# A four-layer graph network on one core: three of four transposes moved from TensorE to VectorE and DRAM, two sums begun on GpSimd, weights loaded by the plan

## The chip, the cores and the metric

The kernel runs on one core of one Trainium2 chip. The metric is the time of one execution in microseconds of device time, the median of several runs. Engines are named as in the profile: PE (TensorE matmuls), PEld (its weight loads), DVE (VectorE), ACT (ScalarE), POOL (GpSimd), SP (SyncE, which here only issues DMAs).

## The reference, cut to what matters

There are 64 independent graphs of 256 nodes with 256 features, and four layers in a row, each of the form `x = layernorm(x + gnn(x, adj))`. All is float32.

```python
# layer 0, 4 heads of 64
att = sigmoid(einsum('bhxd,bhyd->bhxy', q, k) * scale)      # q, k, X: leaky_relu(x @ W)
adj_h = adj[:, None] * att;  deg = sum(adj_h, -1);  dis = where(deg > 0, deg ** -0.5, 0)
Y = einsum('bhxy,bhyd->bhxd', dis[..., :, None] * adj_h * dis[..., None, :], X)    # then layernorm
# layer 1, 8 heads of 32: masked softmax attention, then @ Wo
# layer 2: agg = eps * x + adj @ x;  h = silu(rmsnorm(agg @ W1 + b1));  out = h @ W2 + b2   (1024 hidden)
# layer 3: Wh = x @ W; e = leaky_relu(s1 + s2); out = gelu(layernorm(masked softmax(e) @ Wh))
```

## The kernel before, in words

**Tiles.** One graph's x is a tile of 128 partitions by 512 numbers (two blocks of 128 nodes, side by side). A matmul contracts over partitions, so layers 0, 1 and 3 need x with features on partitions, `xT`. Layer 0 gets it from the input, which is also given transposed. Four times per graph the kernel transposes on PE: `transpose` (L184) issues four 128x128 matmuls against an identity (L189) into PSUM. They are the heads' output of layer 0 (`yT`, L361), x ahead of layer 1 (`xT`, L371), x ahead of layer 3 (`xT3`, L511) and the attention weights of layer 3 (`eT`, L538). `copy` (ACT, L199) fetches a PSUM tile to SBUF. The heads' attention weights of layer 1 go another way already: DVE transposes blocks of 32x32 (L400), SP writes the result to a scratch buffer in DRAM (L402, `far<-eb`) and reads it back in another order with four DMAs (L404, `eT<-far`), in runs of 1 KB.

**Two sums on PE.** Layer 0's degree is a product with a column of ones (L333), over both blocks of nodes of four heads: eight matmuls, packed four side by side in PE's columns. Layer 2's sum of squares is the same (L470), in two runs of four matmuls on the four `sq` tiles that ACT squares (L464).

**A planner.** `graph` records the operations of one graph with an engine, a cost in ns and the tiles they write and read. `Plan.order` sorts the operations of all 64 graphs by list scheduling: the operation that can start first goes next, ties go to the earlier due time. It holds the numbers of buffers per kind (`SLOTS`: 42 of kind `s`, 8 PSUM banks, 8 DRAM buffers), and ACT's functions in turns so that a function table is loaded once per layer and round. `ROUND = 0, 2, 4, 5` says how many rounds behind layer 0 each layer of the same graph runs; about six graphs are under way at any time. The order that results is fixed in the program: each engine, and SP's queue too, runs its instructions in that order and waits on semaphores. A DMA counts 420 ns of SP and lands 4500 ns later in the plan's books.

**Weights** are fetched ahead of the plan by 23 DMAs that ACT issues (`weight`, `row`, `column`, L584 to L621). `c1`, `w3` and `eps_id` are computed from them, `c1` with the program's first matmul (L631).

Of the kernel before, what the change touches and what calls it, by code (L numbers as in the profile page):

```python
# [28 lines left out]
ROUND = 0, 2, 4, 5  # L29
# [3 lines left out]
class Value:  # L33
# [3 lines left out]
    def __init__(self, kind, name, parts=1):  # L37
        self.kind, self.name = kind, name
        self.writer, self.readers = [None] * parts, [[] for _ in range(parts)]
        self.uses, self.slot, self.end, self.t = 0, None, 0.0, None  # L40

# [121 lines left out]

def graph(plan, nc, c, t, out, b):
# [31 lines left out]

    def copy(ps, name):
        dst = Value("s", name, 2)
        op("ACT", 466, lambda: act.copy(dst.t, ps.t), [dst], [ps])  # L199
        return dst  # L200

    def feature_major(w, xT):

        ps = Value("p", "ps", 2)
        for o in range(2):
            def fn(o=o):
                for k in range(DB):
                    pe.matmul(two(ps)[:, o, :], w()[:, k, o * P:(o + 1) * P], two(xT)[:, k, :],  # L208
                              start=(k == 0), stop=(k == DB - 1))
            op("PE", 2 * PE_MM, fn, [(ps, o)], [xT])  # L210
        return ps
# [49 lines left out]
    def plus_row(x, r):  # L261
        xb = Value("s", "xb", 2)
        op("POOL", 1220, lambda: pool.tensor_tensor(two(xb), two(x), row_b(r()), OP.add), [xb], [x])  # L263
        return xb
# [6 lines left out]
    def affine(y, mv, m, g, add, r=(), src=None):  # L271

        src = src or y
        for n in range(NB):
            op("DVE", 395, lambda n=n: dve.scalar_tensor_tensor(
                two(y)[:, n, :], two(src)[:, n, :], m()[:, n, 0:1], g(), op0=OP.subtract, op1=OP.mult),
                [(y, n)], [(src, n), mv])
# [21 lines left out]
    for w, name in ((lambda: c.w0_q, "qT0"), (lambda: c.w0_k, "kT0")):  # L299
# [5 lines left out]
    ps = token_major(xT, lambda: c.w0_l)  # L305
    v = Value("s", "v0")
    op("DVE", 608, lambda ps=ps: dve.tensor_tensor(two(v), two(ps), row_b(c.b0_l), OP.add), [v], [ps])
    op("ACT", 478, lambda: act.activation(v.t, v.t, AF.Prelu, alpha=0.01), [v], [v])
    xb = plus_row(x, lambda: c.b0)
# [18 lines left out]
    ps = Value("p", "ps")  # L328

    def fn(ps=ps):  # L330
        for m in range(NB):
            for h in range(H0):
                pe.matmul(ps.t[h * 32:(h + 1) * 32, :N], c.ones, A(h)[:, m, :], start=(m == 0), stop=(m == NB - 1))  # L333
    op("PE", 2 * PE_MM, fn, [ps], [att], mode="columns")
# [18 lines left out]
    for hp in range(H0 // 2):  # L353
# [7 lines left out]
    ps = transposed(copy(ps, "yT"))  # L361
    y = Value("s", "y", 2)
    op("DVE", 608, lambda ps=ps, y=y: dve.tensor_tensor(by_head(y.t), by_head(ps.t), dis_b(), OP.mult), [y], [ps, dis])
    mv, m = stats(y)
    affine(y, mv, m, lambda: c.g0, lambda n, xb=xb: two(xb)[:, n, :], [xb])
# [5 lines left out]
    xT = copy(transposed(x), "xT")  # L371
    xb = plus_row(x, lambda: c.c1)
    ps = feature_major(lambda: c.w1_q, xT)
    qT1 = Value("s", "qT1")
    op("DVE", 608, lambda ps=ps: dve.tensor_tensor(two(qT1), two(ps), c.b1_q[:, :, None].to_broadcast([P, 2, N]), OP.add),
       [qT1], [ps])

    kT1 = copy(feature_major(lambda: c.w1_k, xT), "kT1")
    v1 = copy(token_major(xT, lambda: c.w1_v), "v1")
# [51 lines left out]
    x = normed(plus(token_major(yT, lambda: c.w1_o), xb), "x2")  # L431

    for n in range(NB):
        d = lambda n=n: two(adjT)[:, n, n * P:(n + 1) * P]
        op("POOL", 418, lambda d=d: pool.tensor_tensor(d(), d(), c.eps_id, OP.add), [(adjT, n)], [(adjT, n)])


    xb = plus_row(x, lambda: c.b2_2)
# [12 lines left out]
    for j in range(0, HB, 2):  # L451
        ps = Value("p", "ps", 2)
        for i in range(2):
            def fn(ps=ps, j=j, i=i):
                for k in range(DB):
                    pe.matmul(two(ps)[:, i, :], c.w2_1[:, k, (j + i) * P:(j + i + 1) * P], two(aggT)[:, k, :],  # L456
                              start=(k == 0), stop=(k == DB - 1))
            op("PE", 2 * PE_MM, fn, [(ps, i)], [aggT])
        both = [(hT, j), (hT, j + 1)]
        for i in range(2):  # L460
            op("ACT", 357, lambda ps=ps, i=i, j=j: act.activation(  # L461
                Hb(j + i)[:, 0], two(ps)[:, i, :], AF.Identity, bias=c.b2_1[:, j + i:j + i + 1]), [(hT, j + i)], [(ps, i)])
# [4 lines left out]
        if len(sqs) == 2:  # L467
            def fn(sqs=sqs, j=j):
                for i in range(4):
                    pe.matmul(sums.t[i * 32:(i + 1) * 32, :N], c.ones, two(sqs[i // 2])[:, i % 2, :],  # L470
                              start=(j == 2), stop=(j == HB - 2))
            op("PE", PE_MM, fn, [sums], [sums, *sqs] if j > 2 else sqs, mode="columns")
            sqs = []
# [17 lines left out]
    for j in range(HB):  # L491
        op("DVE", 391, lambda j=j: dve.scalar_tensor_tensor(  # L492
            Hb(j)[:, 0], Hb(j)[:, 0], c.r2[:, j:j + 1], pr.t[:, :N], op0=OP.mult, op1=OP.mult), [(hT, j)], [(hT, j), pr])
# [5 lines left out]
    for n in range(NB):  # L499
        for half in range(2):  # L500
            js = range(4 * half, 4 * half + 4)

            def fn(ps=ps, n=n, js=js):
                for j in js:
                    pe.matmul(two(ps)[:, n, :], Hb(j)[:, 0, n * P:(n + 1) * P], c.w2_2[:, j, :],  # L505
                              start=(j == 0), stop=(j == HB - 1))
            op("PE", 4 * PE_MM, fn, [(ps, n)], [(hT, j) for j in js] + [(ps, n)] * half)
# [3 lines left out]
    xT3 = copy(transposed(x), "xT3")  # L511
# [3 lines left out]
    for n in range(NB):  # L515
        ps = Value("p", "ps")

        def fn(ps=ps, n=n):
            for k in range(DB):
                pe.matmul(ps.t[:, :D + 2], two(xT3)[:, k, n * P:(n + 1) * P], c.w3[:, k, :],  # L520
                          start=(k == 0), stop=(k == DB - 1))
        op("PE", 2 * PE_MM + 4, fn, [ps], [xT3])
# [19 lines left out]
    affine(y3, mv, m, lambda: c.g3, lambda n: c.b3, src=ps)  # L542
# [7 lines left out]
def gnn_stack_kernel(ctx: ExitStack, tc: tile.TileContext, t: dict, out: bass.AP):  # L550
# [32 lines left out]

    def weight(name):  # L584
        rows, cols = t[name].shape
        w = const.tile([P, rows // P, cols], F32, name=name)
        nc.scalar.dma_start(w, t[name].rearrange("(k p) f -> p k f", p=P))
        return w

    def row(ap, name):  # L590

        r = const.tile([P, ap.shape[0]], F32, name=name)
        nc.scalar.dma_start(r, bass.AP(tensor=ap.tensor, offset=ap.offset, ap=[[0, P], [1, ap.shape[0]]]))
        return r

    def column(ap, name):

        c = const.tile([P, ap.shape[0] // P], F32, name=name)
        nc.scalar.dma_start(c, ap.rearrange("(k p) -> p k", p=P))
        return c  # L600

    w0_q, w0_k, w0_l = weight("L0_gnn_W_q"), weight("L0_gnn_W_k"), weight("L0_gnn_W_lin")
    b0_l = row(t["L0_gnn_b_lin"], "b0_l")
    g0, b0 = row(t["L0_gnn_ln_g"], "g0"), row(t["L0_gnn_ln_b"], "b0")
    w1_q, w1_k, w1_v, w1_o = (weight(f"L1_gnn_W{c}") for c in "qkvo")
    b1_q, b1_v = column(t["L1_gnn_bq"], "b1_q"), column(t["L1_gnn_bv"], "b1_v")
    b1_o = row(t["L1_gnn_bo"], "b1_o")
    w2_1, w2_2 = weight("L2_gnn_W1"), weight("L2_gnn_W2")
    b2_1, r2 = column(t["L2_gnn_b1"], "b2_1"), column(t["L2_gnn_rms_weight"], "r2")
    b2_2 = row(t["L2_gnn_b2"], "b2_2")  # L610
    eps2 = row(t["L2_gnn_epsilon"], "eps2")
    g3, b3 = row(t["L3_gnn_gamma"], "g3"), row(t["L3_gnn_beta"], "b3")
    a3 = row(t["L3_gnn_a"].rearrange("a one -> (a one)"), "a3")


    eps_id = const.tile([P, P], F32, name="eps_id")
    nc.vector.tensor_scalar(eps_id, ident, eps2[:, 0:1], None, op0=OP.mult)


    w3 = const.tile([P, DB, D + 2], F32, name="w3")  # L620
    nc.scalar.dma_start(w3[:, :, :D], t["L3_gnn_W"].rearrange("(k p) f -> p k f", p=P))  # L621
    scratch = const.tile([P, D], F32, name="scratch")
    for k in range(DB):
        for i in range(2):
            nc.vector.scalar_tensor_tensor(scratch, w3[:, k, :D], 1.0, a3[:, i * D:(i + 1) * D], op0=OP.mult,
                                           op1=OP.mult, accum_out=w3[:, k, D + i:D + i + 1])


    ps = pools["p"].tile([P, 512], F32, tag="p", name="ps")[:, :D]
    for k in range(DB):  # L630
        nc.tensor.matmul(ps, b1_v[:, k:k + 1].to_broadcast([P, P]), w1_o[:, k, :], start=(k == 0), stop=(k == DB - 1))  # L631
    c1 = const.tile([P, D], F32, name="c1")
    nc.vector.tensor_tensor(c1, ps, b1_o, OP.add)
    c = SimpleNamespace(**locals())

    plan = Plan()
    for b in range(B):
# [45 lines left out]
```

## Time and profile before

| | |
|---|---|
| median of three runs | 3023.94 us (3023.19 to 3023.97) |
| the profiled execution | 3018.84 us, of which the instructions span 3017.0 us |
| PE / DVE / ACT / POOL busy | 97% / 74% / 67% / 33% of the span |
| DMA packets, mean rate | 305684, 126 GB/s |
| granted PE clock, mean | 0.993 |

The page gives busy shares per engine, then groups of instructions by source line. In a group, "busy" counts the time in which at least one instruction of it runs; "mean" is one instruction's own length. PE's matmuls overlap, so what one costs is read from the start of it to the start of the next. An fp32 matmul is two records in the trace, a transpose is one. "Idle before, releaser" is how long the engine stood still ahead of the group, and who ended it.

### The profile page before, as it was taken

How to read it: one execution, taken by the hardware profiler on the slowest of the kernel's cores; microseconds unless marked ns; L12 is line 12 of the kernel's file. 1: busy time of each engine (PE TensorE's matmuls, PEld its weight loads, DVE VectorE, ACT ScalarE, POOL GpSimd, SP SyncE). 2: the span in 40 equal slices, each digit the busy share in tenths (PEclk: the TensorE clock that was granted, in tenths of full speed). 3: DMA queues.
4: the chain of work that ended last, by engine and by line, in shares of the span. 5: the costliest groups of instructions: out<-in, count | busy, mean ns of one | idle time of the engine just before them, and what ended most of it. 6: DMA issues, size and time to landing. Idle time of an engine off the chain costs nothing.

```text
span 3017.0 us, 57099 instructions
## 1 busy us (share of the span) xinstructions
PE 2925.9 (97%) x19140; PEld 2281.5 (76%) x19140; DVE 2236.8 (74%) x6925; ACT 2019.2 (67%) x4866; POOL 1002.0 (33%) x1286
## 2 busy tenths in 40 slices
PE   6999999999999999999999999999999999999996
PEld 4777777777777777777777777777777877777774
DVE  3778877768777777787687777777777777777864
ACT  2777766776776667676767667667666766677664
POOL 4224333324323333333233323332332333323311
PEclk9999999999999999999999999999999999999998
DMA  5634543534543435434435344344344443553340
GB/s 162 175 102 141 151 123 113 144 105 130 155 131 101 130 109 144 139 118 140 130 95 146 107 134 148 109 137 143 97 133 137 124 126 106 141 141 112 106 126 11
DMA packets 305684, 378.79 MB, mean 126 GB/s; under 512 B 37872, under 2 KB 272240, under 8 KB 305392
## 3 DMA queue, kind: packets, MB, share of 16 engines
q1 hardware_dynamic: 297984, 369.76, 41.9%
q10 hardware_dynamic: 7408, 5.39, 0.6%
q8 instruction: 153, 2.51, 0.4%
q14 instruction: 139, 1.14, 0.1%
HBM read 223.49 MB, written 151.52 MB: 124 GB/s over the span
## 4 chain that ended last, share of the span: by engine, by line
PE 79%; DVE 10%; ACT 6%; DMA 3%; issue 1%; POOL 1%; SPq 0%; ACTq 0%; DVEq 0%; POOLq 0%
PE ps L208 14%; PE ps L219 13%; PE ps L456 12%; PE ps L505 12%; PE ps L388 4%; PE ps L189 3%; PE ps L443 3%; PE ps L358 3%; PE ps L319 3%; PE av L413 3%; PE ps L520 3%; ACT e L292 3%; PE sums L470 2%; DVE st L233 2%; PE ps L333 2%
## 5 line engine op out<-in xcount | busy, mean ns | idle before, releaser
L292 ACT ACTIVATE e<-e,low 128x256 f32<-128x256 f32 x1152 | 583.0, 510 | 67.5 <-DVE low L287 66.9
L456 PE MATMUL ps<-aggT,L_gnn_W 128*128 128x256 f32 x2048 | 487.6, 385 | 1.6 <-ACT aggT L199 1.3
L505 PE MATMUL ps<-L_gnn_W,hT 128*128 128x256 f32 x2048 | 469.0, 383 | 0.3 <-ACT hT L496 0.3
L400 DVE STREAM_TRANSPOSE eb<-e 128x1024 f32<-128x1024 f32 x256 | 316.2, 1237 | 170.5 <-ACT e L292 169.9
L456 PEld LDWEIGHTS ps<-aggT,L_gnn_W 128*128 128x128 f32 x2048 | 377.9, 191 | 81.1 <-issue 24.5
L505 PEld LDWEIGHTS ps<-L_gnn_W,hT 128*128 128x128 f32 x2048 | 385.0, 190 | 70.1 <-issue 19.3
L245 POOL TENSOR_SCALAR mv<-mv 128x2 f32<-128x2 f32 x384 | 125.0, 326 | 905.1 <-DVE mv L235 753.4
L287 DVE CUSTOM_DVE_ANT_0 e<-ps,adj 128x256 f32<-128x256 f32 x1024 | 363.3, 418 | 25.4 <-PE ps L388 25.0
L461 ACT ACTIVATE hT<-ps,b 128x256 f32<-128x256 f32 x512 | 234.2, 471 | 157.9 <-PE ps L456 157.9
L246 POOL TENSOR_TENSOR mv<-mv,mhalf 128x2 f32<-128x2 f32 x384 | 287.6, 749 | 32.0
L263 POOL TENSOR_TENSOR xb<-x,b 128x512 f32<-128x512 f32 x128 | 166.5, 1301 | 281.5 <-DMA x<-in_x 184.8
L233 DVE BATCH_NORM_STATS2 st<-y 128x6 f32<-128x256 f32 x640 | 242.8, 415 | 4.3
L292 ACT ACTIVATION_READ_ACCUMULATOR e<-e,low 128x1 f32 x1152 | 229.8, 199 | 0.0
L492 DVE SCALAR_TENSOR_TENSOR hT<-hT,r,pr 128x256 f32<-128x256 f32 x512 | 205.4, 473 | 20.8 <-PE pr L489 20.5
L326 DVE TENSOR_TENSOR att<-att,adjT 128x512 f32<-128x512 f32 x256 | 170.5, 697 | 21.3 <-ACT att L324 21.3
L256 DVE TENSOR_SCALAR x<-y,mv 128x256 f32<-128x256 f32 x384 | 163.2, 457 | 24.4 <-POOL mv L246 24.0
L484 POOL TENSOR_TENSOR rs<-rs,mhalf 128x2 f32<-128x2 f32 x64 | 46.1, 720 | 377.4 <-DVE rs L483 358.7
L464 ACT ACTIVATE sq<-hT 128x512 f32<-128x512 f32 x256 | 161.9, 633 | 0.3
L496 ACT ACTIVATE hT<-hT 128x1024 f32<-128x1024 f32 x128 | 131.6, 1053 | 40.4 <-DVE hT L492 31.8
L324 ACT ACTIVATE att<-ps 128x512 f32<-128x512 f32 x256 | 132.4, 603 | 27.2 <-PE ps L505 22.4
L346 POOL TENSOR_TENSOR dp<-dp,mhalf 128x8 f32<-128x8 f32 x64 | 107.6, 1682 | 126.1 <-DVE dp L345 119.8
L219 PE MATMUL ps<-v,eT 128*128 128x256 f32 x512 | 141.4, 408 | 8.3 <-ACT eT L199 3.7
(108 smaller groups left out, 5901.1 us busy)
## 6 DMA issues: line engine op xcount, KB each, us to landing
far<-eb SPq DMA_DIRECT2D x256, 512.0 KB, 3.2
eT<-far SPq DMA_DIRECT2D x1024, 128.0 KB, 3.8
x0T<-in_xT SPq DMA_DIRECT2D x64, 256.0 KB, 3.5
adjT<-in_adjT SPq DMA_DIRECT2D x64, 256.0 KB, 3.8
x<-in_x SPq DMA_DIRECT2D x64, 256.0 KB, 3.9
adj<-in_adj SPq DMA_DIRECT2D x64, 256.0 KB, 3.9
rb<-far SPq DMA_DIRECT2D x512, 32.0 KB, 1.9
out<-o SPq DMA_DIRECT2D x64, 256.0 KB, 2.2
```

The lines of the kernel that those rows point to most:

```text
L208: pe.matmul(two(ps)[:, o, :], w()[:, k, o * P:(o + 1) * P], two(xT)[:, k, :], start=(k == 0), stop=(k == DB - 1))
L219: pe.matmul(two(ps)[:, n, :], two(xT)[:, k, n * P:(n + 1) * P], w()[:, k, :], start=(k == 0), stop=(k == DB - 1))
L233: op("DVE", 311, lambda n=n: dve.bn_stats(st.t[:, 6 * n:6 * n + 6], two(src)[:, n, :]), [(st, n)], [(src, n)])
L246: pool.tensor_tensor(m()[:, :, 2], m()[:, :, 2], c.mhalf[:, :NB], OP.pow)
L287: op("DVE", 345, lambda n=n: dve.tensor_tensor_reduce(out=E(n), in0=two(logits)[:, n, :], in1=two(negmask)[:, n, :], scale=-scale, scalar= ...
L292: op("ACT", 491, lambda n=n: act.activation(E(n), E(n), AF.Exp, bias=low.t[:, n:n + 1], scale=-1.0, accum_out=r.t[:, col(n):col(n) + 1]), ...
L326: op("DVE", 608, lambda h=h: dve.tensor_tensor(A(h), A(h), two(adjT), OP.mult), [(att, h)], [(att, h), adjT])
L400: op("DVE", 1130, lambda e=e, eb=eb: dve.transpose(eb.t.rearrange("p (b g i) -> p g b i", b=4, i=32), e.t.rearrange("p (g b i) -> p g b i" ...
L456: pe.matmul(two(ps)[:, i, :], c.w2_1[:, k, (j + i) * P:(j + i + 1) * P], two(aggT)[:, k, :], start=(k == 0), stop=(k == DB - 1))
L461: op("ACT", 357, lambda ps=ps, i=i, j=j: act.activation(Hb(j + i)[:, 0], two(ps)[:, i, :], AF.Identity, bias=c.b2_1[:, j + i:j + i + 1]), ...
L492: op("DVE", 391, lambda j=j: dve.scalar_tensor_tensor(Hb(j)[:, 0], Hb(j)[:, 0], c.r2[:, j:j + 1], pr.t[:, :N], op0=OP.mult, op1=OP.mult), ...
L505: pe.matmul(two(ps)[:, n, :], Hb(j)[:, 0, n * P:(n + 1) * P], c.w2_2[:, j, :], start=(j == 0), stop=(j == HB - 1))
```

## The change

1. `yT`, `xT` and `xT3` no longer go through PE and ACT's `copy`, but through `far_transposed`: one DVE transpose of 32x32 blocks (of `yT` straight from PSUM), a write to DRAM, four DMAs back. For `yT` it is one write of 2 KB rows and four reads in runs of 512 B, and the rows' order within the tile is left permuted: the multiplication by `dis` that follows (two instructions of 256 numbers now, one of 512 before) puts it right. For `xT` and `xT3` it is four writes in runs of 512 B and four reads in runs of 128 B. `eT` of layer 3 stays on PE.
2. POOL adds pairs of tiles ahead of the two sums: two additions per graph for the degree, two for the sum of squares. PE then does four matmuls in place of eight for each.
3. The weights are operations of the plan and are issued by SP between the inputs' loads, by due time; no DMA is left on ACT.
4. `ROUND` is 0, 2, 5, 7.

```diff
-ROUND = 0, 2, 4, 5
+ROUND = 0, 2, 5, 7
...
+def weights(plan, nc, c, t):
...
+    def weight(name, key, rows=D, cols=D):
+        v = const(name, [P, rows // P, cols])
+        op("SP", rows * cols // 200 + 420, lambda: nc.sync.dma_start(
+            v.t, t[key].rearrange("(k p) f -> p k f", p=P)), [v], after=3500)
...
+    def far_transposed(src, name, in_order=True):
+
+
+        eb, far, dst = Value("s", "eb"), Value("h", "far", 4), Value("s", name, 4)
+        op("DVE", 600, lambda: dve.transpose(
+            eb.t.rearrange("p (b g i) -> p g b i", b=4, i=32),
+            src.t.rearrange("p (n k w) -> p k n w", n=2, k=2)), [eb], [src])
+        if in_order:
+            F = lambda a: far.t[:64].rearrange("(a z) (y w) -> a (z y) w", a=4, w=P)[a]
+            for a in range(4):
+                op("SP", 420, lambda a=a: nc.sync.dma_start(
+                    F(a).rearrange("(b j) w -> j b w", b=4),
+                    eb.t[32 * a:32 * a + 32].rearrange("j (b w) -> j b w", b=4)), [(far, a)], [eb], after=3000)
+            for a in range(4):
+                op("SP", 420, lambda a=a: nc.sync.dma_start(
+                    dst.t.rearrange("q (g a i) -> a q g i", g=4, a=4)[a],
+                    F(a).rearrange("q (g i) -> q g i", g=4)), [(dst, a)], [(far, a)], after=4500)
+            return dst
+        op("SP", 420, lambda: nc.sync.dma_start(far.t[:, :512], eb.t), [(far, i) for i in range(4)], [eb], after=3000)
+        for q in range(4):
+            op("SP", 420, lambda q=q: nc.sync.dma_start(
+                dst.t[32 * q:32 * q + 32].rearrange("j (a g) -> j a g", a=4),
+                far.t[:, :512].rearrange("(a j) (b g) -> b j a g", a=4, b=4)[q]), [(dst, q)],
+                [(far, i) for i in range(4)], after=4200)
+        return dst
...
+    added = [Value("s", "added") for _ in range(H0 // 2)]
+    for i in range(2):
+        A2 = lambda n, i=i: att.t.rearrange("p (h n c) -> p h n c", h=H0, n=NB)[:, 2 * i:2 * i + 2, n]
+        op("POOL", 1220, lambda i=i, A2=A2: pool.tensor_tensor(two(added[i]), A2(0), A2(1), OP.add),
+           [added[i]], [(att, 2 * i), (att, 2 * i + 1)])
...
-        for m in range(NB):
-            for h in range(H0):
-                pe.matmul(ps.t[h * 32:(h + 1) * 32, :N], c.ones, A(h)[:, m, :], start=(m == 0), stop=(m == NB - 1))
-    op("PE", 2 * PE_MM, fn, [ps], [att], mode="columns")
+        for h in range(H0):
+            pe.matmul(ps.t[h * 32:(h + 1) * 32, :N], c.ones, two(added[h // 2])[:, h % 2], start=True, stop=True)
+    op("PE", PE_MM, fn, [ps], added, mode="columns")
...
-    ps = transposed(copy(ps, "yT"))
+    yb = far_transposed(ps, "yT", in_order=False)
...
-    xT = copy(transposed(x), "xT")
+    xT = far_transposed(x, "xT")
...
+        if len(sqs) % 2 == 0:
+            op("POOL", 1220, lambda a=sqs[-2], sq=sq: pool.tensor_tensor(sq.t, sq.t, a.t, OP.add), [sq], [sq, sqs[-2]])
...
-    xT3 = copy(transposed(x), "xT3")
+    xT3 = far_transposed(x, "xT3")
```

More of the change, by code (lines that the diff above doesn't have):

```diff
@@ L262, in plus_row @@
         xb = Value("s", "xb", 2)
-        op("POOL", 1220, lambda: pool.tensor_tensor(two(xb), two(x), row_b(r()), OP.add), [xb], [x])
+        op("POOL", 1220, lambda: pool.tensor_tensor(two(xb), two(x), row_b(r.t), OP.add), [xb], [x, r])
         return xb
@@ L370, in graph @@
     negmask = adj
[L371 to L373 removed]
+    xT = far_transposed(x, "xT")
+    xb = plus_row(x, c.c1)
+    ps = feature_major(c.w1_q, xT)
     qT1 = Value("s", "qT1")
[L375 to L379, printed above, removed]
+    op("DVE", 608, lambda ps=ps: dve.tensor_tensor(two(qT1), two(ps), c.b1_q.t[:, :, None].to_broadcast([P, 2, N]), OP.add),
+       [qT1], [ps, c.b1_q])
+    kT1 = copy(feature_major(c.w1_k, xT), "kT1")
+    v1 = copy(token_major(xT, lambda: c.w1_v.t, [c.w1_v]), "v1")
     av, r = Value("p", "av", 2), Value("c", "r")
@@ L465, in graph, with fn @@
         sqs.append(sq)
[L467 to L473, printed above, removed]
+        if len(sqs) % 2 == 0:
+            op("POOL", 1220, lambda a=sqs[-2], sq=sq: pool.tensor_tensor(sq.t, sq.t, a.t, OP.add), [sq], [sq, sqs[-2]])
+    def fn(sqs=sqs):
+        for i in range(4):
+            pe.matmul(sums.t[i * 32:(i + 1) * 32, :N], c.ones, two(sqs[i // 2 * 2 + 1])[:, i % 2, :],
+                      start=True, stop=True)
+    op("PE", PE_MM, fn, [sums], [sqs[1], sqs[3]], mode="columns")
     part = Value("s", "part")
@@ L602, in gnn_stack_kernel @@
[L602 to L632, printed above, removed]
@@ L633, in gnn_stack_kernel @@
-    nc.vector.tensor_tensor(c1, ps, b1_o, OP.add)
-    c = SimpleNamespace(**locals())
+    c = SimpleNamespace(const=const, ident=ident, ones=ones, mean_of=mean_of, mhalf=mhalf)
     plan = Plan()
+    weights(plan, nc, c, t)
     for b in range(B):
```

108 lines of the change are left out of this document (73 added, 35 removed).

## The prediction

> **What bounds the kernel now.** I read the page first: busy shares, then the chain of work that ended last.
>
> ```profile
> PE 2925.9 (97%) x19140; PEld 2281.5 (76%) x19140; DVE 2236.8 (74%) x6925; ACT 2019.2 (67%) x4866; POOL 1002.0 (33%) x1286
> ...
> PE 79%; DVE 10%; ACT 6%; DMA 3%; issue 1%; POOL 1%; SPq 0%; ACTq 0%; DVEq 0%; POOLq 0%
> ```
>
> PE is busy almost throughout and the chain runs over it, so what is taken off PE should come off the time, as far as no other queue takes its place. Next, busy time by stretches (columns: us, then PE, PEld, DVE, ACT, POOL busy with instruction counts, granted clock, DMA share, GB/s):
>
> ```profile
> 0.00:40.00 40.00, 11.45 (x42) 9.20 (x44) 0.83 (x5) 4.81 (x7) 16.60 (x16) 0.88 0.94 289
> 40.00:60.00 20.00, 20.00 (x136) 15.34 (x134) 13.48 (x27) 9.70 (x19) 11.48 (x10) 0.99 0.10 34
> 60.00:2900.00 2840.00, 2806.32 (x18521) 2190.32 (x18518) 2164.60 (x6708) 1941.55 (x4707) 956.49 (x1229) 1.00 0.44 127
> 2900.00:3005.00 105.00, 87.99 (x450) 66.60 (x449) 52.32 (x169) 62.49 (x134) 15.54 (x27) 0.91 0.17 51
> 3005.00:3017.00 12.00, 0.14 (x1) 0.00 (x0) 5.57 (x18) 0.63 (x1) 1.86 (x4) 0.50 0.06 23
> ```
>
> PE stands still 28.6 us of the first 40, 33.7 of the 2840 between, and 28.9 of the last 117. DMA has room in the middle, none at the start. Then PE's timeline, where a line's cost is the distance to the next line's start:
>
> ```profile
> 1616.10 0.30 PE L189 MATMUL ps<-ident,x 128*128 128x128 f32 x1 [0.80 <-DVE x L256]
> 1616.93 0.55 PE L189 MATMUL ps<-ident,x 128*128 128x128 f32 x3 [0.53 <-DVE x L256]
> ...
> 1621.03 1.05 PE L333 MATMUL ps<-att,ones 128*32 128x256 f32 x16
> 1622.01 0.66 PE L189 MATMUL ps<-ident,x 128*128 128x128 f32 x4
> 1622.50 0.60 PE L189 MATMUL ps<-ident,yT 128*128 128x128 f32 x4
> 1622.94 0.38 PE L341 MATMUL ps<-ident,deg 128*128 128x128 f32 x2
> ```
>
> Four transposes of x cost 0.49 us here (mean of all 128 runs 0.52, waits apart), four of yT 0.44, the degree's sum 0.98. From the groups and the DMA view:
>
> ```profile
> L189 PE MATMUL ps<-ident,x 128*128 128x128 f32 x512 | 84.1, 282 | 23.4 <-DVE x L256 23.2
> L400 DVE STREAM_TRANSPOSE eb<-e 128x1024 f32<-128x1024 f32 x256 | 316.2, 1237 | 170.5 <-ACT e L292 169.9 <-DMA rb<-far 0.2
> L256 DVE TENSOR_SCALAR o<-y,mv 128x256 f32<-128x256 f32 x128 | 63.9, 541 | 17.8 <-POOL mv L246 17.8
> L413 PE MATMUL av<-eT,v 128*32 128x256 f32 x2048 | 125.5, 382 | 0.0
> far<-eb SPq DMA_DIRECT2D x256, 512.0 KB, 3.2
> eT<-far SPq DMA_DIRECT2D x1024, 128.0 KB, 3.8
> ```
>
> The first row's 23.2 us are PE waiting for DVE ahead of x's transposes. L413, which reads tiles that went through DRAM, never waited: the plan's 4500 ns cover the 3.8 us measured.
>
> **PE, work removed.** Transposes of x: 128 x 0.52 = 66 us. Of yT: 64 x 0.44 = 28. Degree: half of eight matmuls is two of four packed passes of 216 ns (the start-to-start median of a 256-column record), 64 x 0.43 = 28. Sum of squares: one of two runs goes. A run of eight records takes 0.58, and the matmul ahead of it takes 309 ns in place of 216, so 64 x 0.67 = 43. Sum **165 us**, all on the path. The 23 us of waiting at L189 go too; their successor is below.
>
> **Start, moved.** Before, PE's first matmul waits 18.4 us for `b_v`, and ACT issues weights until 34.8, so its first activation comes then. After, SP issues `W_q`, `W_k` and three x0T first; `W_q` landed 3.8 us after issue before, so PE starts near 5. Against that, all 23 weight loads now stand in SP's queue: the first `yT` write is 47th in its order, and 11.6 MB at the 289 GB/s above take 40 us. Until layer 1's first matmul, the order holds 56 us of layer 0 on PE, and that matmul can hardly come before 70. I take 18 us idle for 28.6, a gain of **10**, with ends 25 and -10.
>
> **End.** The last graph's x now takes the way through DRAM ahead of layer 3 with nothing beside it: DVE 0.6, last write issued 1.4 later (three issues of 0.48, start to start), landing 3.2, last read 3.8, together 9.1, for 2 us of transposes and copy; one POOL addition (1.3) ahead of the sum of squares; and two more rounds between layer 0 and layer 3 leave PE less to do beside the last chains. A chain some 8 longer plus about 11 us of cover lost: **19 us**, ends 5 and 45.
>
> **DVE.** Added: 192 transposes of half of L400's 1.24, 119 us (yT's reads PSUM, which no transpose here does yet; L363 reads as much from there in 0.68, so at most 4 more), and 10 to 18 for the split multiplication. POOL gets 256 additions of 1.30 (row of L263), 333 us, to 1335, under half the span. They hurt DVE: L256 has a median of 407 ns but a mean of 541 and a longest of 1395, and the long ones lie beside POOL's 1.3 us operations. Such excess sums to some 51 us now over 383 us of POOL's long operations; 333 more bring 44. DVE comes to 2410 of 2860 us, 84%: not the bound. The Trainium skill (SBUF — State Buffer, SBUF: two separate sides) says that GpSimd and a two-port DVE operation exclude each other for a whole instruction, which is what L256 shows; by that rule, if each new addition held DVE for half its length, an estimate of 166 us in place of 44, DVE would stand at 89%. ACT loses 192 copies of 0.58, 112 us.
>
> **DMA and SP.** Per graph there are 21 DMAs more: 5760 data packets, 4096 of them of 128 B, 1536 of 512 B, 128 of 2 KB. The packet records of before have 9.4 ns for loads of 4 B, 32.9 for 512 B, 60.6 for 1 KB and 180 for 4 KB (means). A 128 B packet lies between 9.4 and, far off, 60.6; I take 18, nearer the first two. Then the 128 B runs add 295 us per engine (154 to 993), the rest 260; with today's 1297 the DMA share is 65% (60 to 89%). Here the Trainium skill speaks against the change (DMA: Bandwidth & Descriptors, Specifications): under 512 B the engine does a read-modify-write. The 4 B loads at 9.4 ns do not show that; if such a packet cost twice the 512 B one, an estimate of 66 ns, the share would be about 92%. SP issues 55 DMAs per graph for 34, 25 us at today's 0.39 to 0.48; with waits for landings, some 4.7 pairs of write and read per graph with little between, 32 of 44.6 us. Nothing is gained by issue time; it must stay hidden.
>
> **New waits.** What counts is PE work standing, in the new order, between a chain's matmul and the matmul that reads its result (counted at 216 ns per record). From layer 0's attention product over yT, two normalizations and xT to layer 1's first product: 34 to 35 us. By rows the chain is 9.1 (DRAM) + 8.1 (16 DVE and 4 POOL steps) + 9.1 (DRAM) = 26.3; the middle part is the multiplication 0.9, statistics 2 x 1.2, POOL 2 x 1.1, scale and add 1.9, scaling 0.8. For x3: 18 to 21 us against 3.8 + 9.1 = 12.9. Before, x3's chain of 3.8 had 5.3 to 6.1 and still caused most of the 23 us, so queueing on DVE eats about 2 us per such chain, and about 5 of x1's. That leaves x1's 3.3 us and x3's 3 to 6. Only tails should stall: I take twice today's 23, **46**, ends 0 and 170 (below).
>
> **Sum.** 3018.8 (profiled run) - 165 - 23 - 10 + 19 + 46 = 2886; the median of the runs lies 5 above the profiled one: **2890 us**.
>
> **Rivals.**
> *A, forecast*, PE stays the bound: 2850 to 2925. Chance 0.58.
> *B, landings lengthen a little.* x1's chain passes four landings. If each takes between 0.85 and 1.5 us more than 3.2 and 3.8, the 3.3 us are used up and each graph stalls for up to 4 x 1.5 - 3.3 = 2.7 us, 173 us in all: 2925 to 3017, middle 2970. For: SP's queue is in order, and a write waiting for DVE holds all reads behind it. Against: the new DMAs are light (0.3 to 0.7 us of the engines each, for 1.44 of an `eb` write). Chance 0.17.
> *C, slower.* The same chain becomes the bound: from about 1.5 us more per landing (5.3 where eT's median is 3.8 and its longest 6.9) the stalls exceed all that PE saved. At 2 us more, 64 x (4 x 2 - 3.3) = 301 us on top of the 2845 without waits: 3146. For: in the first 40 us, at a DMA share of 0.94, x0T landed up to 8.7 after issue. Against: it needs 128 B packets near 60 ns, which would bring the share to 89%. Chance 0.15.
> *D, the waits vanish and the start gains 25*: 2830 to 2850. Chance 0.07.
> *E, the change does not do what it says.* In the new order the records of L189 on x and yT are gone and the sums are halved, so it can only be that waits eat just that much: 3018 to 3030, chance 0.03.
>
> The range takes A, B and half of D: **2840 to 3015**. Faster by over 0.2% (about what a measurement of this kernel can tell from no change) 0.82, within it 0.03, slower 0.15.
>
> **What would show it.** PE busy near 2750 us; no L189 on x and yT; the two sums at half their records; PE's first matmul near 5 us; DVE's share near 84%; DMA near 65%, 128 B packets near 18 ns. Wrong would be: reads of 128 B landing over 5 us, PE waiting for DMA xT for more than 100 us in sum, or idle PE beyond 60 us at the end.

## The result, and the profile after

The change takes **3184.07 us** (median of four runs, 3177.18 to 3188.14) where the kernel before, on the same chip, takes 3023.95: ratio 1.0527 [1.0508, 1.0545]. It was forecast at 2890 and is slower by 5%. (One kernel further below, `weights`, ran slow while it was profiled, 3381.7 us at a granted clock of 0.845 where its nine other runs take about 3028, so its trace is not read.) The page of the changed kernel, busy times and the chain that ended last:

```profile
span 3182.6 us, 56140 instructions
...
PE 2898.6 (91%) x17348; PEld 2218.9 (70%) x17348; DVE 2467.2 (78%) x7181; ACT 1937.4 (61%) x4676; POOL 1326.8 (42%) x1542
...
PE 48%; DMA 16%; DVE 13%; ACT 9%; SPq 6%; POOL 4%; issue 2%; DVEq 0%; POOLq 0%; ACTq 0%
```

PE has 1792 records fewer, as planned, but only 27 us less busy time, and stands idle 284.0 us (span less busy) where it stood 91.1. DMA now carries 16% of the chain. Which wait it is, the list of PE's waits says (waiting line and tile, releaser: us in total, times, longest):

```profile
PE ps L303 <- DMA x0T<-in_xT: 127.6, 27, 6.0
PE sums L576 <- POOL sq L572: 33.0, 27, 1.7
PE ps L625 <- DMA xT<-far: 13.5, 4, 9.4
PE ps L432 <- POOL added L427: 13.0, 5, 6.1
```

The largest is not a transposed tile. It is `x0T`, layer 0's input, which is loaded as before: a load that the change does not touch. The same matmuls as groups of lines, in the kernel before, after, and (ahead of its turn) in the best mended version, `books_l12`:

```profile
L208 PE MATMUL ps<-x0T,L_gnn_W_q 128*128 128x256 f32 x512 | 126.5, 386 | 0.2 <-DMA x0T<-in_xT 0.2
```

```profile
L303 PE MATMUL ps<-x0T,w_q 128*128 128x256 f32 x512 | 173.2, 485 | 127.6 <-DMA x0T<-in_xT 127.6
```

```profile
L303 PE MATMUL ps<-x0T,w_q 128*128 128x256 f32 x512 | 129.8, 391 | 8.0 <-DMA x0T<-in_xT 8.0
```

Two things changed in the middle row: the idle time ahead, and the busy time itself (173.2 for 126.5) for the same 512 records. One of the 27 stalls shows both. SP's queue and PE, from the timeline of the changed kernel:

```profile
2056.12 6.75 SPq L508 DMA_DIRECT2D eT<-far  x10
2062.98 0.40 SPq L651 DMA_DIRECT2D out<-o  x1
2063.42 2.89 SPq L508 DMA_DIRECT2D eT<-far  x6
2066.41 0.40 SPq L250 DMA_DIRECT2D adj<-in_adj  x1
2066.85 0.47 SPq L250 DMA_DIRECT2D x0T<-in_xT  x1
```

```profile
2066.13 0.27 PE L524 MATMUL ps<-ident,r 128*16 128x128 f32 x1
2071.67 2.04 PE L303 MATMUL ps<-x0T,w_q 128*128 128x256 f32 x4 [5.26 <-DMA x0T<-in_xT]
```

The load is issued at 2066.85, when PE already stands: the next matmul in its order is the one that reads this tile, and it starts 4.8 us later. Then four records span 2.04 us, where eight of the same size, at 1025.62 in this trace, span 1.99. The stretches (columns as in the prediction) say why:

```profile
2066.40:2071.60 5.20, 0.01 (x1) 0.00 (x0) 2.28 (x9) 2.84 (x6) 0.60 (x1) 0.75 1.01 255
2071.60:2076.00 4.40, 4.33 (x14) 3.80 (x15) 1.61 (x7) 0.00 (x0) 2.69 (x3) 0.52 0.01 2
```

The granted clock (the column before the last two) is 0.52 in the 4.4 us after the wait. Over the whole run it is granted at half for 252 us, in 40 spells; before it was 47 us in 6. A spell begins in the wait or just behind it, so only a part of it falls on busy PE. The 20 waits of 4 to 7 us between 200 and 2850 us are 5.2 us long in the mean, and the half clock behind each takes another 2.5: a wait of 5 us costs between 7 and 8. The 27 waits for x0T thus cost 127.6 us and, by the 24 spells that go with them, 62 more.

**The account.** Idle PE grew by 193 us. Over the whole span the clock's loss, (1 - mean granted clock) x span, grew from 21 (0.993) to 124 us (0.961), but half clock costs nothing while PE stands: what falls on busy PE grew from 12 to 96 us, by 84. What is left of PE's busy time, its work at full clock, fell from 2914 to 2803 us, by 112, where the prediction took off 165. Together 193 + 84 - 112 = 165; the span grew by 166. The records that went or were halved cost 231 us at full clock before and 84 after, 147 less; the other records take 35 us more, which I could not place.

### The profile page after: what moved, and what is told of

Its sections match the earlier page's. It is cut to its first block, busy times and chain, and to the rows that moved or that the text cites. A ratio compares the mean times of both kernels' runs of the same rounds, so it can differ in the third digit from the quotient of the medians.

```text
span 3182.6 us, 56140 instructions
## 1 busy us (share of the span) xinstructions
PE 2898.6 (91%) x17348; PEld 2218.9 (70%) x17348; DVE 2467.2 (78%) x7181; ACT 1937.4 (61%) x4676; POOL 1326.8 (42%) x1542
## 4 chain that ended last, share of the span: by engine, by line
PE 48%; DMA 16%; DVE 13%; ACT 9%; SPq 6%; POOL 4%; issue 2%; DVEq 0%; POOLq 0%; ACTq 0%
PE ps L303 11%; PE ps L610 7%; PE ps L314 7%; PE ps L560 5%; DMA x0T<-in_xT 4%; ACT e L387 4%; DVE eb L504 3%; SPq L508 3%; DMA out<-o 3%; PE ps L492 3%; PE ps L457 3%; PE av L517 2%; DVE att L421 2%; PE ps L625 2%; PE ps L547 2%
## 5 line engine op out<-in xcount | busy, mean ns | idle before, releaser
L610 PE MATMUL ps<-w,hT 128*128 128x256 f32 x2048 | 494.2, 390 | 13.0 <-ACT hT L601 12.8
L560 PE MATMUL ps<-aggT,w 128*128 128x256 f32 x2048 | 472.2, 383 | 11.0 <-DVE dis L446 9.5
L610 PEld LDWEIGHTS ps<-w,hT 128*128 128x128 f32 x2048 | 378.1, 191 | 115.7 <-issue 32.7
L560 PEld LDWEIGHTS ps<-aggT,w 128*128 128x128 f32 x2048 | 384.5, 190 | 82.2 <-DVE dis L446 13.4
L303 PE MATMUL ps<-x0T,w_q 128*128 128x256 f32 x512 | 173.2, 485 | 127.6 <-DMA x0T<-in_xT 127.6
L421 DVE TENSOR_TENSOR att<-att,adjT 128x512 f32<-128x512 f32 x256 | 227.9, 927 | 30.5 <-DMA adjT<-in_adjT 29.2
L572 POOL TENSOR_TENSOR sq<-sq 128x512 f32<-128x512 f32 x128 | 172.0, 1344 | 157.0 <-ACT sq L568 157.0
L427 POOL TENSOR_TENSOR added<-att 128x512 f32<-128x512 f32 x128 | 175.3, 1378 | 135.4 <-DVE att L421 51.1
L303 PEld LDWEIGHTS ps<-x0T,w_q 128*128 128x128 f32 x512 | 118.9, 245 | 154.5 <-issue 120.5
L403 ACT ACTIVATE v<-v 128x512 f32<-128x512 f32 x64 | 40.3, 630 | 273.6 <-DVE v L402 176.2
```

Source lines behind the costliest of these rows:

```text
L303: pe.matmul(two(ps)[:, o, :], w.t[:, k, o * P:(o + 1) * P], two(xT)[:, k, :], start=(k == 0), stop=(k == DB - 1))
L421: op("DVE", 608, lambda h=h: dve.tensor_tensor(A(h), A(h), two(adjT), OP.mult), [(att, h)], [(att, h), adjT])
L560: pe.matmul(two(ps)[:, i, :], c.w2_1.t[:, k, (j + i) * P:(j + i + 1) * P], two(aggT)[:, k, :], start=(k == 0), stop=(k == DB - 1))
```

## The experiments

All are the change with the edit named, unless said otherwise. "Idle" is the span less PE's busy time, "clock" is (1 - mean granted clock) x span, both of the profiled execution, in us; a part of "clock" lies over idle PE and costs nothing. Where parts of the change are named, all else is as before, the rounds included.

| run | edit | us | ratio to before, 95% | idle | clock |
|---|---|---|---|---|---|
| (before) | | 3023.9 | | 91 | 21 |
| (the change) | | 3184.1 | 1.0527 [1.0508, 1.0545] | 284 | 124 |
| x0t_const | layer 0 waits for no load | 3063.0 | 1.0126 [1.0106, 1.0146] | 208 | 67 |
| left_12 | LEFT 12 | 3027.0 | 1.0004 [0.9992, 1.0016] | 202 | 73 |
| x0t_act | x0T issued by ACT | 3214.6 | 1.0628 [1.0603, 1.0654] | 286 | 135 |
| round_0245 | rounds as before | 3087.5 | 1.0212 [1.0175, 1.0250] | 225 | 102 |
| weights | part 3 alone | 3028.0 | 1.0009 [0.9999, 1.0019] | | |
| pool_only | parts 2 and 3 alone | 2932.5 | 0.9691 [0.9677, 0.9706] | 78 | 26 |
| yt_only | yT's way and part 3 | 3040.4 | 1.0049 [1.0031, 1.0068] | 121 | 43 |
| x_only_l12 | x's two ways, part 3, LEFT 12 | 3005.2 | 0.9932 [0.9915, 0.9950] | 123 | 51 |
| l12_no_pool | LEFT 12, sums on PE | 3008.8 | 0.9945 [0.9930, 0.9960] | 139 | 51 |
| l12_no_deg | LEFT 12, degree on PE | 3023.2 | 0.9996 [0.9984, 1.0008] | 178 | 73 |
| pool_x1_l12 | parts 2, 3, one way, LEFT 12 | 2933.9 | 0.9695 [0.9678, 0.9712] | 96 | 41 |
| pool_x3_s45 | parts 2, 3, the other way | 2938.3 | 0.9713 [0.9696, 0.9730] | 93 | 38 |
| s45 | 45 buffers | 3057.7 | 1.0112 [1.0086, 1.0139] | 221 | 82 |
| s53 | 53 buffers | 2961.4 | 0.9789 [0.9771, 0.9807] | 148 | 56 |
| books | two measured prices | 3010.2 | 0.9957 [0.9942, 0.9972] | 157 | 69 |
| loads_l12 | one price, LEFT 12 | 2965.4 | 0.9817 [0.9800, 0.9833] | 153 | 44 |
| books_l12 | two prices, LEFT 12 | 2929.2 | 0.9685 [0.9669, 0.9701] | 121 | 41 |
| books_s45_l13 | prices, 45 buffers, LEFT 13 | 2935.0 | 0.9712 [0.9698, 0.9727] | 128 | 50 |

### First set: is it the late loads?

Theories: **LATE LOADS**, the order issues x0T too late; **QUEUE**, SP's in-order queue is late as a whole and x0T only the first to show it; **DVE**, POOL's additions slow DVE. The plan's own times for its order speak for the first. They hold the first use of an x0T 59 us after its issue (median) before, and 12 us after the change; 27 of the 64 are under 6 us, as many as PE's waits. The traces agree: 63 and 14 us, with 1 and 26 of 64 under 6. The plan's books count 60 ns for issuing an input's load and 3000 to its landing (the 420 and 4500 given further above hold for `far` and `eT`); the DMA view says, for the kernel after:

```profile
far<-eb SPq DMA_DIRECT2D x512, 64.0 KB, 1.8
xT<-far SPq DMA_DIRECT2D x512, 64.0 KB, 2.6
x0T<-in_xT SPq DMA_DIRECT2D x64, 256.0 KB, 5.2
```

and for the kernel before:

```profile
x0T<-in_xT SPq DMA_DIRECT2D x64, 256.0 KB, 3.5
```

The new ways land early; the old load takes 5.2 us where it took 3.5.

QUEUE has a part in it too. For the late loads the plan has 3.3 us from issue to use; in the trace PE begins to stand 0.3 us after the issue (mean of 26 waits). So of a wait of 4.9 us about 1.9 is a landing that takes longer than in the books, and about 3.0 is the issue, which comes that much closer to PE's use than planned. Ahead of an x0T load SP now issues 13 DMAs back to back in 7.5 us (medians; 1 in 0.5 us before): in the fence above ten reads of eT take 6.75 us, 4.2 by the books.

**x0t_const.** Layer 0's three projections read one fixed tile, so PE waits for no x0T.

```diff
-        ps = feature_major(w, xT)
+        ps = feature_major(w, xT, c.still)
```

> The changed kernel (3184 us), with every engine's order as it is and every DMA still issued, but layer 0's three projections read one tile that was loaded once at the start in place of each graph's x0T, so this part of the computation is changed and PE no longer waits for the x0T loads. In the changed kernel PE stood still 127.6 us in 27 waits for x0T, and the granted clock was 0.5 for 252 us, nearly all of it just after such waits (6.8 us after each of 27: about 92 us lost). Theory LATE LOADS (too few buffers of kind s, so the plan loads x0T only just in time, and the load lands later than the plan's books): 3184 - 128 - 92 = 2964, PE waits below 130 us in all, clock above 0.985. Rival QUEUE (SP's in-order queue as a whole runs late, and the next thing in it takes the place of x0T): 3090 to 3150, with new waits of PE for xT or eT. Rival DVE (additions of POOL slow DVE, which sets the pace): 3130 to 3184.

3063.0, between LATE LOADS and QUEUE: 121 us back. The waits for x0T are gone, but 52 us of a wait that was at 2.4 come up (L594, for POOL's `rs`, 27 times): some of what stood behind the loads was late too. Of the half clock 92 us were expected to go with these waits; it was 62 (above).

**left_12.** Loads are operations with nothing ahead of them, and such an operation starts only while `LEFT` buffers stay free. The bounces (the ways through DRAM) hold buffers of kind `s` (`eb` and the tile read back), and so do `added` and the `sq` that wait for POOL.

```diff
-LEFT = 16
+LEFT = 12
```

> The changed kernel with one number changed: the plan keeps 12 buffers of kind s free ahead of a load instead of 16, so that loads start earlier (in the plan's order 7 of 64 x0T loads stand less than 6 us before their use, 27 in the changed kernel). LATE LOADS: most of the 220 us of waits and slow clock go: 2980 to 3030. QUEUE: loads are still behind the reads of eT in SP's order: 3120 to 3180. DVE: 3130 to 3184.

3027.0, as LATE LOADS has it: 157 us back by one number. QUEUE and DVE, each alone, put it at 3120 or more. By the plan's times 7 loads of 64 are under 6 us ahead. PE's largest waits:

```profile
PE ps L524 <- DVE r L522: 36.2, 18, 3.8
PE ps L303 <- DMA xT<-far: 19.3, 9, 4.6
```

**x0t_act.** The loads go by ACT's queue.

> The changed kernel with the 64 loads of x0T issued by ACT instead of SP, at the same place of the overall order; all other orders are as they were. LATE LOADS: the plan still puts each load just ahead of its use, so the landing (5.2 us measured, 3.06 in the books) still shows: 27 waits of 2 to 3 us in place of 4.7, 3080 to 3130. QUEUE: x0T no longer stands behind 16 reads of eT, and the waits for it nearly go: 2970 to 3010. DVE: 3130 to 3184.

3214.6, slower, and outside all three ranges. x0T's wait falls to 32.8, but L303 and L524 now wait 109 us for ACT. So it does not separate QUEUE from LATE LOADS: ACT was the wrong place.

**round_0245.** `ROUND` as before the change.

> The changed kernel with the rounds of before, 0, 2, 4, 5: fewer graphs under way, so buffers come free earlier, but less to do beside the longer chains. If the wider rounds are what costs: below 3000. LATE LOADS with the tiles that the bounces and the additions hold as the cause: no better than the changed kernel, 3150 to 3300, since 25 of 64 loads of x0T still stand less than 6 us before their use in the plan's order.

3087.5: neither. x0T's waits fall to 23.8 us (9 times), others take their place. By the plan 25 loads are still under 6 us ahead, but here they land in 3.6 us (median), not 5.2: a short lead does not by itself make a load late. The wider rounds cost about 97 of the 160 us. That more graphs under way hold more buffers is a likely reason, not a shown one.

### Second set: what is each part worth alone?

After left_12, the suspicion was **LOCK**: POOL's additions hold up DVE (the product with adjT has a mean of 697 ns before, 927 after, at a median of 685).

> Only the third part of the change: the kernel before with its weights issued by the plan on SP (and PE's transposes, sums and rounds as before). Theories by now: LOADS (the x0T loads are issued too late in the order, and each wait of 4 to 6 us is followed by a spell of half clock), LOCK (POOL's additions hold DVE up, and the chains over DVE come late). Neither puts a cost here: in this order 2 of 64 x0T loads are issued less than 6 us ahead of their use, as before. Both expect 3005 to 3018, the start of PE moved from 18 us to about 6, less what PE then waits for the other weights. A rival, START: the 23 loads in SP's queue push the first graphs' loads back, and the start loses what it gained: 3020 to 3035.

3028.0: no gain, START's number. In `pool_only`, with the same start, PE's first matmul comes at 6.2 us. What eats the gain shows in `yt_only` (below), which has the same start and its sums on PE:

```profile
PE ps L453 <- DVE v L446: 20.7, 3, 17.6
```

One wait of 17.6 us, from 35 to 52 us: POOL waits 8.9 us for a graph's x, whose load stands behind weights in SP's queue, and the step on POOL that this `v` needs comes behind that in POOL's order. In `x_only_l12` and `l12_no_pool` the same wait is 16.6 and 16.1 us.

> The second and third parts of the change: POOL's additions and the planned weights; all transposes on PE, rounds 0, 2, 4, 5, LEFT 16. PE loses 71 us of work by the prediction's terms (28 for the degree, 43 for the sum of squares). If the additions cost nothing elsewhere: 71 below the run with weights alone, 2935 to 2955. By LOADS: 10 of 64 x0T loads are issued under 6 us ahead in this order; at 4.7 us of wait and 2 to 3 us of half clock each, 65 to 75 us, so 3000 to 3025, with 40 us or more of waiting of PE for x0T. By LOCK: 256 additions cost DVE about 140 us beside 71 saved on PE, so 3010 to 3070, and PE's waits are for DVE and POOL tiles, not for x0T; DVE's two-input operations have means 80 us or more above their medians in sum.

2932.5, just below the range for additions that cost nothing elsewhere. LOADS, which put it at 3000 or more for 10 late loads, misses here: PE waits 13.4 us for x0T. **LOCK falls**: the additions pay 92 us on the kernel before, more than the prediction gave them. In the page and waits of `pool_only`:

```profile
PE 2847.5 (97%) x18116; PEld 2258.8 (77%) x18116; DVE 2315.0 (79%) x6925; ACT 2010.0 (69%) x4866; POOL 1317.0 (45%) x1542
```

```profile
PE ps L303 <- DMA x0T<-in_xT: 13.4, 7, 6.2
PE ps L258 <- DVE x L351: 12.5, 11, 3.4
```

PE is 78 us less busy and still at 97%. The same additions that make 33 us of waiting at the sum of squares in the change make none here.

> yT alone through DRAM, and the planned weights; x's transposes and the sums on PE as before, rounds 0, 2, 4, 5, LEFT 16. One x0T load of 64 is issued under 6 us ahead. LOADS and LOCK both leave the gain standing: 28 us of PE work less than the run with weights alone, and some waits: 2975 to 2995. QUEUE (SP's queue late as a whole with any way through DRAM): 3020 or more, with PE waiting for y's chain or for loads.

3040.4: slower than the weights alone, where 28 us were to be gained. QUEUE's number, though its waits are small: x ahead of PE's transposes 33.9 us (23.2 before), and the half clock 43 for 21. Against the kernel before, idle PE grew by 30 us, of which 17.6 are the wait at the start. Why it is slower than the weights alone I do not know.

> The change with LEFT 12 (3027.0 us with it) and without POOL's additions: both sums on PE as before; three transposes through DRAM, planned weights, rounds 0, 2, 5, 7. PE gets 71 us of work back. By LOCK the additions cost more than they save: 2985 to 3010, with POOL waits gone and DVE's two-input operations back near their medians. If the additions pay as forecast: 3085 to 3100. By LOADS alone (4 of 64 x0T loads late in this order, as against 7 with the additions): 3070 to 3090.

3008.8, inside LOCK's range; but pool_only has shown LOCK wrong in its general form. So the three ways through DRAM with sums on PE gain 16 us where 94 were to be gained, and adding POOL's additions to them (3027.0) loses 18 where it gains 96 beside the weights alone. The parts are not additive: singly they add up to about 2921.

### Third set: together or alone?

**SLOTS**: buffers too few for all parts at once. **PAIR**: bounces pay, except beside the additions. **CHAINS**: bounces do not pay.

```diff
-SLOTS = {"s": 42, "d": 10, "b": 3, "c": 72, "p": 8, "h": 8}
+SLOTS = {"s": 45, "d": 10, "b": 3, "c": 72, "p": 8, "h": 8}
```

> The change with 45 buffers of kind s in place of 42; LEFT 16 and all else as in the change (3184.1 us). The bounces hold buffers of this kind (eb and the tile read back), so do the tiles that POOL adds, and a load may only start while 16 are kept free. SLOTS (too few buffers make the x0T loads late): in this order 5 of 64 x0T loads are issued under 6 us ahead, 27 in the change, 7 with LEFT 12, so the time falls to that of LEFT 12, 3015 to 3060, with under 40 us of PE waiting for x0T. If the loads are late for SP's queue and not for buffers: 3140 or more, with 20 or more waits for x0T.

3057.7: three buffers give 126 us. PE's waits for x0T, in this run and in left_12:

```profile
PE ps L303 <- DMA x0T<-in_xT: 12.2, 4, 6.1
```

```profile
PE ps L303 <- DMA x0T<-in_xT: 14.4, 5, 6.3
```

**Too few buffers make the plan put the loads late** is shown, from both sides.

> x's two transposes through DRAM and the planned weights; yT's transposes and both sums on PE, rounds 0, 2, 4, 5, LEFT 12; one x0T load late in this order. PE loses 66 us of work. PAIR (a way through DRAM pays by itself, and it is with POOL's additions, which hold DVE and the buffers, that the chains come late): 2960 to 2995. CHAINS (the ways through DRAM bring waits that eat what they take off PE, whatever POOL does; yT alone gave 3040 where the weights alone gave 3028): 3010 to 3050.

3005.2, between the two ranges and nearer to CHAINS': 23 us off the weights alone, for 66 forecast.

> The change with LEFT 12 (3027.0 us) and the degree's sum on PE as before; POOL still adds for the sum of squares, all three transposes through DRAM; 7 of 64 x0T loads late, as with LEFT 12. PE gets 28 us back. PAIR by way of DVE: the degree's additions run beside DVE's products of att and adjT, whose mean is 834 ns with LEFT 12 and 726 without POOL's additions; that goes, and the time falls to 2990 to 3015. If the additions for the degree do no harm: 3045 to 3060. If it is the other pair that does the harm (PE waits for the sum of squares): 3030 to 3060 with those waits unchanged.

3023.2, between the ranges. PE has 28 us of work more and the kernel takes no longer: beside the ways through DRAM the degree's additions cost about what they save (idle PE is 178 us, 202 with them). The excess of DVE's operations over their medians falls, from 218 us in sum to 147; that this is the cause is not shown.

> POOL's additions and the planned weights (2932.5 us with these alone), LEFT 12, and one way through DRAM, that of x ahead of layer 1; x ahead of layer 3 and yT stay on PE, rounds 0, 2, 4, 5; one x0T load late. PE loses another 33 us. PAIR in its strong form (any bounce beside the additions comes late): 2940 to 2980. SLOTS (only more bounces than the buffers carry come late; this one has its loads 85 us ahead in the median): 2895 to 2920. CHAINS: 2930 to 2960, with PE's waits for xT over 30 us.

2933.9, no gain on 2932.5: CHAINS' number, but without the wait for xT that it names; 96 us of idle PE for 78, and 41 us of clock for 26.

### Fourth and fifth set: buffers or prices?

Open was why all parts together with LEFT 12 take 3027 and not 2921. **BOOKS**: the order is made on wrong prices.

> The change with 53 buffers of kind s, LEFT 16. The room comes from weights: layer 0's three and layer 1's four projections each use one weight tile, and layer 2's second product uses the first one's tile in another shape, so seven weight loads fall away and the products are computed with other numbers; every instruction after the start is as in the change. In this order 1 of 64 x0T loads is issued under 6 us ahead, the median 55 us ahead (12 in the change, 59 before). The parts taken singly add up to about 2921 (additions -96, yT +12, x -23, weights +4); with LEFT 12 the change takes 3027, with 45 buffers 3058. SLOTS in its strong form (what the parts lose together is lost to buffers): 2900 to 2960. BOOKS or QUEUE (prices of the plan, or SP's queue, make the chains late whatever the buffers): 2990 to 3035, with waits of PE for r, xT, yT and added as with LEFT 12.

2961.4, just past the upper end of SLOTS. With 11 buffers more (room that only a kernel with shared weights has) the change would pay 63 us as it was planned; what of it is due to the seven loads fewer at the start was not measured.

```diff
-        op("SP", 60, lambda: nc.sync.dma_start(two(v), ...), [v])
+        op("SP", 480, lambda: nc.sync.dma_start(two(v), ...), [v], after=5500)
...
-                op("SP", 420, lambda a=a: nc.sync.dma_start(
+                op("SP", 670, lambda a=a: nc.sync.dma_start(
                     dst.t.rearrange("q (g a i) -> a q g i", g=4, a=4)[a],
```

> The change with LEFT 12 (3027.0 us) and two measured prices in the plan's books: an input's load counts 480 ns of SP and lands 5500 ns later (60 and 3000 in the change; measured 5.2 us in the median for x0T), a read of xT or xT3 counts 670 ns of SP (420; measured 672 from start to start). BOOKS (the order is made on wrong prices, so chains that it holds for hidden come late): 2940 to 2995. SLOTS or QUEUE (the order is about as good as buffers and queue let it be): 3010 to 3045; the plan's own sum of PE's idle stretches grows from 4.5 to 12 us with these prices.

**2929.2**, below BOOKS' range: 98 us from two prices in the plan. No operation is added or taken away, only the order differs. Its page:

```profile
PE 2809.5 (96%) x17348; PEld 2183.5 (75%) x17348; DVE 2467.2 (84%) x7181; ACT 1939.4 (66%) x4676; POOL 1335.1 (46%) x1542
```

DVE is busy for the very 2467.2 us of the change.

> POOL's additions and the planned weights (2932.5 us with these alone), 45 buffers of kind s, LEFT 16, and one way through DRAM, that of x ahead of layer 3; x ahead of layer 1 and yT on PE, rounds 0, 2, 4, 5. 33 us of PE work less; the bounce ahead of layer 1 gave 2933.9 in its place, no gain. SLOTS: with the loads 71 us ahead in the median and this bounce the shorter chain to hide by the plan, 2895 to 2920. CHAINS (a bounce gives back what it takes off PE, in waits, in half clock, and at the end of the last graph): 2925 to 2945.

2938.3: CHAINS. Neither way of x pays by itself beside the additions.

> The change with the two measured prices alone (an input's load 480 ns of SP and 5500 ns to its landing, a read of xT or xT3 670 ns of SP), LEFT 16, 42 buffers. In this order 1 of 64 x0T loads is issued under 6 us ahead (27 in the change), but only 7.6 us ahead in the median, and the plan's own sum of PE's idle stretches is 41 us, where it was 2.6. BOOKS (with LEFT 12 these prices took the time from 3027 to 2929): the late loads and the late chains go, less what the plan now leaves idle itself: 2960 to 3000. SLOTS (LEFT 16 leaves too few buffers for any order): 3050 or more.

3010.2: the prices alone mend 174 of the change's us, though LEFT 16 leaves too few buffers for a good order; SLOTS' 3050 is missed. This is 10 above BOOKS' range. PE's waits for x0T:

```profile
PE ps L303 <- DMA x0T<-in_xT: 12.8, 7, 6.0
```

> LEFT 12 and the loads' price alone (480 ns of SP, landing 5500 ns later); reads of xT and xT3 stay at 420 ns. 1 of 64 x0T loads late. If the loads' price is what matters: 2920 to 2945, as with both. If it is the price of the 512-packet reads on SP, 8 per graph and 2 us more per graph than the books have: 2995 to 3025, with waits of PE for xT, r and yT as with LEFT 12. If both carry a part: 2945 to 2990.

2965.4, both carry a part: 62 us by the loads' price, 36 by that of the reads.

> Both prices, 45 buffers of kind s, LEFT 13: the order with the plan's shortest span and least idle PE (2.6 us). If the remaining waits with both prices and LEFT 12 (gap of PE 0.9 us per graph) are a matter of buffers: 2885 to 2920. If not: 2922 to 2940.

2935.0: no better. What is left, 128 us of idle PE with the start and the end, is not a matter of these buffers.

## Why the prediction was wrong, point by point

**The step that failed is "New waits".** It asked how much PE work covers the two chains that the change makes longer, and took 46 us, at most 170, for their stalls. Those chains held: PE waits 18.6 us for xT in both places together (L303 5.1, L625 13.5). Nothing was asked about operations that the change does not touch. Before, a load was issued 59 us ahead of use by the plan's times, so that it made no difference that the plan held it for landed after 3 us (the page of before has 3.5). The change puts three more `eb` per graph and the additions' tiles into the same 42 buffers and holds the transposed tiles longer. Loads then start when enough buffers come free, just in time by the plan's books, and about 5 us late on the chip. One term, the wait for loads, was 0 in the sum and measured 127.6 us; a second, the half clock that goes with these waits, was 0 and measured 62. A third, smaller, was 0 as well: PE waits 46 us for POOL's additions (L576 33.0, L432 13.0), whose cost to the chains was counted for the last graph alone. More buffers, fewer kept free and right prices, each alone, took PE's waits for x0T down to between 12 and 15 us; the time came to 3058, 3027 and 3010. By the same step "Nothing is gained by issue time; it must stay hidden" left out that a read in 512 runs takes SP 672 ns from start to start (median), where I counted 390 to 480.

**PE work, 165.** The records are gone as said, but PE's work at full clock fell by 112 us in the change and 136 in books_l12, and busy PE, forecast near 2750, is 2899. The additions' 71 were 78 by busy time and 92 by time in pool_only. The ways' 94 came to little: in books_l12 PE is only 38 us less busy than in pool_only (2809.5 for 2847.5), since other records take longer, and 42 more idle (121 for 78). So the 38 us that are left were paid back in waits.

**23 us at L189** went. **Start, gain 10**: the first matmul comes at 6.0 us, forecast near 5, and PE's idle in the first 100 us fell from 28.6 to 18.6, just the forecast; but over the first 200 it grew from 29.7 to 33.3, and the weights alone gain nothing. **End, loss 19**: idle in the last 117 us is 34.3 for 28.9, so 5.

**DVE** is busy 2467 us (2410 forecast), **POOL** 1327 (1335). In pool_only DVE runs the 6925 operations of before and is busy 78 us longer (2315.0 for 2236.8), between the 44 that were forecast for the additions and the 166 of the estimate beside it. At 78% DVE bounds nothing, and in books_l12 it has the forecast 84%.

**DMA.** The queue's share is 56% (65% forecast), a packet of 128 B takes 13.0 ns (18 forecast), reads of xT land in 2.6 us. The Trainium skill (DMA: Bandwidth & Descriptors, Specifications) says that under 512 B the engine does a read-modify-write. It gives no price; my estimate of twice a 512 B packet, 66 ns, would have had the share near 92%. At 13.0 ns, with 32.2 for 512 B, no trace of this case shows such a price.

**Rivals.** C gave 3146 and the right sign by luck, since its mechanism did not take place: the landings of its chain came early (1.8 to 2.6 us where 3.2 and 3.8 were counted), and those of `eT` and its `far` stayed (4.0 for 3.8, 3.0 for 3.2). The landing that lengthened, x0T's, is not on that chain. B falls likewise. The signs of wrong that I named (reads over 5 us, 100 us of waiting for xT, 60 us idle at the end) all stayed away; the time was lost at a place that none of them watched.

**Open.** The 35 us of PE time in the account; how much of the late loads is SP's queue and how much the landing; why yT alone is slower; and what the last 120 us of idle PE in books_l12 would need. Whether another queue than SP's or ACT's would carry the ways better was not tried, and neither was pool_only with the right prices.

## What to carry to other kernels

Where a planner fixes the order, a part that shares buffers with others changes the order of everything that takes a buffer: look how far ahead of use each load stands in the new order, in particular those that the change does not touch, and compare that with the measured landing. Price a load in the plan at what the trace shows, since a wrong price costs little while there is slack (the plan of before has the same) and much when the slack goes. And try the parts one by one: here POOL's two pairs of additions are the whole gain (2932.5), and the three ways through DRAM, even well ordered (2929.2), add what a measurement can hardly tell.

## What the runs showed of the hardware that I had not expected

PE's clock falls to half in or after a wait, and not for long waits only. Between 200 and 2850 us of the changed kernel, a spell of half clock went with all 20 waits of 4 to 7 us, 4 of 5 of 3 to 4 us, 2 of 3 of 2 to 3, and 3 of 32 of 1 to 2 us; spells last 3.4, 6.8 or 10.2 us. The Trainium skill (TensorE: Matmul & The Clock Gate, Part 1: The HAM clock gate) says nearly the same: an idle window of about 3.4 us halves the clock, and about as long a busy one restores it. The lengths of the spells agree; the 5 spells that went with waits under 3 us are more than that rule says. So idle PE has two prices, and several waits of 1.5 us are cheaper than one of 5: books_l12 has 42 us more idle PE than pool_only and 15 more of clock loss, while the change has 193 more than before and 103 more of clock loss.
